# Attention's weighted sums as two column-tile products of 128x64 instead of one product of 128x128

## The chip, the core and the metric

The kernel runs on one core of a Trainium2 chip. A core has five engines with an instruction stream each: TensorE (PE in the profile, with its weight loads listed apart as PEld), VectorE (DVE), ScalarE (ACT), GpSimd (POOL) and SyncE (SP). TensorE multiplies with an array of 128 rows by 128 columns: a weight load puts a stationary matrix of up to 128x128 into it, and a MATMUL streams the columns of a second matrix through it and writes or adds the product to PSUM. The array can also be addressed as smaller tiles; a product is then told which rows and columns of the array it uses. The metric is the device time of one execution in microseconds (us), the median over runs.

## The reference, cut to what matters

One block of group norm, attention over the 32x32 pixels of an image, a projection and a residual, in float32, for 16 images of 512 channels:

```python
xn = group_norm(x, 8 groups)                              # x: (16, 512, 32, 32)
qkv = einsum('oc,bchw->bohw', qkv_w, xn) + qkv_b
q, k, v = to_heads(split(qkv, 3))                         # 4 heads of 128, n = 1024 pixels
attn = softmax(einsum('bhnd,bhmd->bhnm', q, k) * 128 ** -0.5)
out = einsum('bhnm,bhmd->bhnd', attn, v)
return x + einsum('oc,bchw->bohw', proj_w, out) + proj_b
```

The change concerns the einsum that makes `out`.

## The kernel before, in words

**Attention.** The work goes through 16 images x 4 heads x 8 key blocks of 128 pixels: 512 steps. A step has two halves of 512 query pixels. `scores` (product in L846) multiplies a key block with half of the queries, which gives scores transposed: key pixels on the partitions, 512 queries along them. ScalarE takes their exponential into the tile `p` (L852), without subtracting a maximum. `weighted_sum` (product in L942), one step later, multiplies the block of V (128 key pixels by 128 channels of the head, the stationary matrix) with the half of `p` (the streamed matrix, 512 columns) and accumulates over the 8 key blocks in `po`, a PSUM tile of 128 channels by 1024 queries. After the eighth block ScalarE copies `po` out (L949). VectorE adds the `p` tiles up (L860) for the softmax's denominators, which are divided out of the copied result later.

**V's block.** `v_block` returns it. For the first image its 128 channels lie next to each other. From the second on V comes in a layout in which the channels of one block are four elements apart: `v[:, j // n, h % 2, :, j % n]` with n = 4.

**The other products.** Q, K, V and the projection are made by two levels of Strassen's method: products of 128x128 weights with 256 streamed columns (L606; `qk_x`, `qk_y`, `v_x`, `v_y`, `pp_x`, `pp_y` in the profile) whose results are copied and added by ScalarE and VectorE. The last image's projection has one level, with 512 columns (L1031; `lx`, `ly`, `lz`).

**The order.** Python lists of such units are spread over the eight steps of a head (`plan_head`): while a head's attention runs, the projection of the image before or the Q, K or V of the next one is made between the products of the attention. In the loop at the end of `fast_path` a half step issues `scores`, then `weighted_sum` of the step before, then half of the step's units; a scheduler orders each engine's stream under the dependencies from there, so that a product of L846, one of L942 and some of L606 usually alternate on TensorE.

**Other tile shapes.** At the end a check of the softmax's range makes two products with one column and one streamed element: L1077 (32 rows) uses a 32x32 tile of the array and L1078 (128 rows) a tile of 128x32; both write `most`. All else uses 128x128. A general path for inputs out of that range is in the program and is not run here.

Of the kernel before, what the change touches and what calls it, by code (L numbers as in the profile page):

```python
# [16 lines left out]
P = 128  # L17
# [169 lines left out]
def fast_path(ctx, tc, x, sources, out, consts, flag, dims):  # L187
# [6 lines left out]
    nc = tc.nc  # L194
    B, C, N, NCC, NH2, NB, GC, SCALE = dims
# [597 lines left out]
    def v_block(b, h, j):  # L793
        v, n = vs[b, h // 2], NB // NH2
        return v[:, h % 2, j, :] if b == 0 else v[:, j // n, h % 2, :, j % n]
# [39 lines left out]
    ps, tot, po, rinv, last_eviction = {}, {}, {}, {}, {}  # L835
# [3 lines left out]
    def where(s):  # L839
        bh, j = divmod(s, NB)  # L840
        return (*divmod(bh, HEADS), j)
# [95 lines left out]
    def weighted_sum(s, half):  # L937
        b, h, j = where(s)
        if j == 0 and half == 0:
            po[b, h] = ps_o.tile([P, N], F32, tag="o", name=f"po_{b}_{h}")  # L940
        i = ts(half, HALF)
        nc.tensor.matmul(  # L942
            po[b, h][:, i], v_block(b, h, j), ps[s][:, i],
            start=(j == 0), stop=(j == NB - 1),
        )
        if j == NB - 1:
            if (b, h) not in os_:
                os_[b, h] = opool.tile([P, N], F32, tag="o", name=f"o_{b}_{h}")
            last_eviction[b] = nc.scalar.copy(os_[b, h][:, i], po[b, h][:, i])  # L949
# [291 lines left out]
    for s in range(steps + 1):  # L1241
        units = []
        if s < steps:
            b, h, j = where(s)
            if j == 0:
                plan = plan_head(b, h)
            units = plan[j]
            if j == NB - 1 and h == 2 and b + 1 < B:
                next_v.append(v_groups(b + 1))
                next_qk.append(qk_groups(b + 1, 1))  # L1250
                units.append(ahead[f"v_{b + 1}"])
        if NB < s < steps and s % NB == 1:
            denominators(*where(s - 2)[:2])
        for half in range(NH2):
            if s < steps:
                scores(s, half)
                if j in (1, 2) and half == 1 and s > NB:
                    with tc.issue_after(exps[s].ins):
                        spread_inverse(*where(s - NB)[:2], j - 1)
                if half == 1 and j == 4 and s > NB:  # L1260

                    with tc.issue_after(added[b, h, 4].ins):
                        divide(*where(s - NB)[:2])
            if s > 0:
                weighted_sum(s - 1, half)
            n = (len(units) + 1) // 2
            run(units[half * n : (half + 1) * n])
        if s > 0:
            del ps[s - 1]
# [134 lines left out]
```

## Time and profile before

| | |
|---|---|
| time, median of 2 runs | 3171.86 us (3171.75 to 3171.98) |
| span of the profiled execution | 3170.7 us |
| VectorE busy | 2633.6 us, 83% |
| ScalarE busy | 1439.7 us, 45% |
| probabilities L852, ScalarE, 1024 of 128x512 | 597 ns each |
| adding up L860, VectorE, 385 of 128x1024 | 1218 ns each |
| L606 products qk_x with qk_t, rows of 256 columns | 1344, 382 ns each |
| granted TensorE clock | full, in all of 40 slices |

The profile is of one execution. An f32 product shows as two MATMUL rows and two weight loads, so that the 1024 products of L942 are 2048 rows. A matmul's row lasts from its start to its modelled end, which lies after the start of the next; the distance of starts, and not the length of a row, is what a product takes of TensorE. In the groups of part 5 the columns are line, engine, operation, output <- inputs, array rows*columns, shape and type, count, then busy us and mean ns, then the engine's idle time before them and what ended it. The chain of part 4 is followed back from the last instruction to what released each step.

### The profile page before, as it was taken

To read this page: it belongs to the slowest core of one execution; us is meant where nothing else is said; L and a number is where in the kernel's file an instruction comes from. 1 tells how busy PE (TensorE), PEld (TensorE's weight loads), DVE (VectorE), ACT (ScalarE), POOL (GpSimd) and SP (SyncE) were. 2 spreads that over 40 slices of the span, in tenths; PEclk is the share of its full clock that TensorE was granted. 3 is DMA by queue.
4 is the path that set the end of the run, shared out by engine and by line. 5 is a ranking of instruction groups with operands and counts; after the bars stand their busy time and mean duration, and the time that the engine had idled before them with its cause. 6 is when DMAs were issued, how large, how long until landed. Compare 5 with 4: busy or idle time off the path is not lost.

```text
span 3170.7 us, 34267 instructions
## 1 busy us (share of the span) xinstructions
PE 3159.9 (100%) x10524; PEld 2190.7 (69%) x10524; DVE 2633.6 (83%) x4639; ACT 1439.7 (45%) x2712; POOL 517.7 (16%) x898
## 2 busy tenths in 40 slices
PE   9999999999999999999999999999999999999999
PEld 7566676677766676777767767677676776766764
DVE  9878879788897888878788787987879978788784
ACT  3535435354353543545435453453534545344342
POOL 0011221111211112211122111222012221122200
PEclk9999999999999999999999999999999999999999
DMA  5554554555545455454554545555455564555531
GB/s 177 185 190 154 188 172 154 171 153 192 171 164 162 153 185 175 167 167 145 191 172 162 171 145 187 171 172 172 144 175 169 176 189 134 174 162 186 179 116 41
DMA packets 210333, 524.32 MB, mean 165 GB/s; under 512 B 32096, under 2 KB 65376, under 8 KB 210144
## 3 DMA queue, kind: packets, MB, share of 16 engines
q1 hardware_dynamic: 132896, 282.12, 28.8%
q0 software_dynamic: 64000, 204.54, 19.2%
q10 hardware_dynamic: 13248, 35.39, 3.5%
q8 instruction: 87, 1.43, 0.2%
q14 instruction: 102, 0.84, 0.1%
HBM read 388.77 MB, written 133.17 MB: 165 GB/s over the span
## 4 chain that ended last, share of the span: by engine, by line
PE 96%; DVE 3%; DMA 0%; issue 0%; POOL 0%; SPq 0%; ACT 0%; DVEq 0%; POOLq 0%
PE po L942 27%; PE s L846 27%; PE qk_x L606 12%; PE qk_y L606 9%; PE pp_x L606 6%; PE v_x L606 6%; PE pp_y L606 4%; PE v_y L606 4%; PE lx L1031 0%; DVE qk_t L574 0%; PE ly L1031 0%; PE warm L1153 0%; DVE tot L860 0%; DVE qk L714 0%; DVE qk_r L630 0%
## 5 line engine op out<-in xcount | busy, mean ns | idle before, releaser
L942 PE MATMUL po<-p,v 128*128 128x512 f32 x2048 | 1049.5, 594 | 0.7 <-ACT p L852 0.7
L846 PE MATMUL s<-qk,qk 128*128 128x512 f32 x2048 | 1047.4, 593 | 0.3 <-DVE qk L714 0.3
L852 ACT ACTIVATE p<-s 128x512 f32<-128x512 f32 x1024 | 610.9, 597 | 961.0 <-PE s L846 957.2
L942 PEld LDWEIGHTS po<-p,v 128*128 128x128 f32 x2048 | 603.6, 302 | 322.7 <-issue 214.5
L860 DVE TENSOR_TENSOR tot<-tot,p 128x1024 f32<-128x1024 f32 x385 | 469.0, 1218 | 158.4 <-ACT p L852 156.3
L846 PEld LDWEIGHTS s<-qk,qk 128*128 128x128 f32 x2048 | 387.7, 190 | 88.6 <-issue 29.9
L606 PEld LDWEIGHTS qk_x<-qk_t,w 128*128 128x128 f32 x1344 | 251.8, 190 | 166.1 <-issue 75.3
L606 PE MATMUL qk_x<-qk_t,w 128*128 128x256 f32 x1344 | 356.3, 382 | 0.1
L486 ACT COPY qk_u<-qk_x 128x512 f32<-128x512 f32 (+1 forms) x256 | 136.3, 533 | 229.2 <-PE qk_x L606 229.2
L779 POOL DMA_DIRECT2D vd<-vu x120 | 66.7, 557 | 899.8 <-DVE vu L771 897.9
L630 DVE TENSOR_TENSOR qk_r<-qk_y,qk_u 128x512 f32<-128x512 f32 (+1 forms) x256 | 157.7, 616 | 34.7 <-ACT qk_u L486 21.6
L580 POOL DMA_DIRECT2D kept_t<-qk_t x240 | 129.4, 540 | 278.4 <-DVE qk_t L574 211.9
L606 PEld LDWEIGHTS pp_x<-pp_t,w_proj 128*128 128x128 f32 x630 | 117.2, 190 | 74.7 <-issue 32.3
L784 POOL DMA_DIRECT2D v<-vd x240 | 140.6, 593 | 167.1 <-DMA vd<-vu 70.3
L630 DVE TENSOR_TENSOR v_r<-v_y,v_u 128x512 f32<-128x512 f32 (+1 forms) x120 | 76.0, 633 | 110.6 <-ACT v_u L486 80.3
L606 PE MATMUL pp_x<-pp_t,w_proj 128*128 128x256 f32 x630 | 167.8, 383 | 0.0
L606 PE MATMUL v_x<-v_t,w_v 128*128 128x256 f32 x630 | 166.6, 381 | 0.0
L830 POOL DMA_DIRECT2D out_y<-y x120 | 66.0, 550 | 604.2 <-DVE y L829 602.4
L606 PEld LDWEIGHTS v_x<-v_t,w_v 128*128 128x128 f32 x630 | 118.4, 190 | 55.3 <-issue 19.1
L606 PE MATMUL qk_y<-x,w 128*128 128x256 f32 x512 | 142.1, 379 | 0.0
L714 DVE SCALAR_TENSOR_TENSOR qk<-qk_r,qkb_sb,qk_r 128x512 f32<-128x512 f32 x192 | 137.5, 743 | 1.6
L486 ACT COPY v_u<-v_x 128x512 f32<-128x512 f32 (+1 forms) x124 | 66.3, 535 | 157.1 <-PE v_x L606 130.3
(217 smaller groups left out, 4487.2 us busy)
## 6 DMA issues: line engine op xcount, KB each, us to landing
w<-kept SPq DMA_DIRECT2D x90, 512.0 KB, 3.7
kept_t<-qk_t POOLq DMA_DIRECT2D x180, 256.0 KB, 3.3
v_t<-kept_t SPq DMA_DIRECT2D x180, 256.0 KB, 2.9
w<-kept SPq DMA_DIRECT2D x90, 384.0 KB, 3.4
rinv<-row ACTq DMA_DIRECT2D x63, 512.0 KB, 4.9
x<-in_x POOLq DMA_DIRECT2D x60, 512.0 KB, 4.6
vd<-vu POOLq DMA_DIRECT2D x120, 256.0 KB, 3.1
v<-vd POOLq DMA_DIRECT2D x240, 128.0 KB, 4.2
```

The source lines that it names most:

```text
L486: nc.scalar.copy(t[n][:, :width], t["x"][:, :width])
L580: nc.gpsimd.dma_start(t, to)
L606: nc.tensor.matmul(acc[:, ts(i, Q)], have["w"][t][:, i, slot, :], inner(i, bn), start=(first and i == 0), stop=True, skip_group_check=True,)
L630: nc.vector.tensor_add(dst, view(a), view(c))
L714: nc.vector.scalar_tensor_tensor(st[b, h][:, ts(half, HALF)], a, qkb_sb[:, i : i + 1], c, ALU.add, ALU.add)
L779: nc.gpsimd.dma_start(rows[which][ts(h, P), :], u)
L784: nc.gpsimd.dma_start(vs[b, pair][ts(q, BLK), half].rearrange("m h (k i) j -> m (h k) (i j)", k=n), rows[which].rearrange("(k m) (q e) -> ...
L830: nc.gpsimd.dma_start(out[b, ts(o, P), ts(half, HALF)], t)
L846: nc.tensor.matmul(sc, ks[b, h][:, ts(j, P)], qs[b, h][:, ts(half, HALF)], start=True, stop=True)
L852: exps[s] = nc.scalar.activation(ps[s][:, ts(half, HALF)], sc, AF.Exp, scale=SCALE)
L860: added[b, h, j] = nc.vector.tensor_add(tot[b, h][:, i], tot[b, h][:, i], ps[s][:, i])
L942: nc.tensor.matmul(po[b, h][:, i], v_block(b, h, j), ps[s][:, i], start=(j == 0), stop=(j == NB - 1),)
```

## The change

`weighted_sum` takes the 128 channels of V's block as two halves of 64. Each half is a product of its own: 128 rows by 64 columns of weights, the same 512 streamed columns, and the lower or upper 64 partitions of the same stretch of `po`. The first half is placed on the array's columns 0 to 63, the second on 64 to 127. Starts and ends of the accumulation are as before, for each half by itself.

```diff
         i = ts(half, HALF)
-        nc.tensor.matmul(
-            po[b, h][:, i], v_block(b, h, j), ps[s][:, i],
-            start=(j == 0), stop=(j == NB - 1),
-        )
+        v = v_block(b, h, j)
+        for d in range(2):
+            cols = ts(d, P // 2)
+            nc.tensor.matmul(
+                po[b, h][cols, i], v[:, cols], ps[s][:, i],
+                start=(j == 0), stop=(j == NB - 1),
+            )
         if j == NB - 1:
```

In the program built from it the two halves of a product stand next to each other on TensorE in 1009 of 1024 cases; in 15 the scheduler puts another product between them (L606, once L88). The line of the product becomes L945, and later lines move by three. The other engines have the same instructions as before.

## The prediction

> **What bounds the kernel now.** I read four views, from the whole to the single instruction. First the page: the busy shares (its part 1), the chain that ended last (part 4), and the two groups of the attention in part 5.
>
> ```profile
> PE 3159.9 (100%) x10524; PEld 2190.7 (69%) x10524; DVE 2633.6 (83%) x4639; ACT 1439.7 (45%) x2712; POOL 517.7 (16%) x898
> ...
> PE po L942 27%; PE s L846 27%; PE qk_x L606 12%; PE qk_y L606 9%; PE pp_x L606 6%; PE v_x L606 6%; PE pp_y L606 4%; PE v_y L606 4%; PE lx L1031 0%; DVE qk_t L574 0%; PE ly L1031 0%; PE warm L1153 0%; DVE tot L860 0%; DVE qk L714 0%; DVE qk_r L630 0%
> ...
> L942 PE MATMUL po<-p,v 128*128 128x512 f32 x2048 | 1049.5, 594 | 0.7 <-ACT p L852 0.7
> L846 PE MATMUL s<-qk,qk 128*128 128x512 f32 x2048 | 1047.4, 593 | 0.3 <-DVE qk L714 0.3
> ```
>
> The reader is to see that TensorE (PE) alone sets the end: it has work all the time, po, the line that is changed, carries 27% of the chain, and in the whole run it waited 0.7 us for its probabilities. Nothing that lengthens po can hide. There are 1024 weighted products (16 images, 4 heads, 8 key blocks, 2 halves) and 2048 rows: an f32 product is two passes here, each a weight load and a MATMUL.
>
> A row of 594 ns is not what a pass costs, since passes overlap. The chain in order of time (start, length) gives the pitch:
>
> ```profile
> 1500.28 0.86 PE s L846 x2
> 1501.13 0.95 PE pp_x L606 x4
> 1502.08 0.87 PE po L942 x2
> 1502.95 0.86 PE pp_y L606 x4
> ```
>
> Two passes over 512 columns take 0.86 us, so one takes 0.43; four over 256 take the same, so 0.215: the time goes with the streamed columns, and the other 0.16 us of a row lies under the next pass. Check: 2048 x 0.43 = 881 us is 27.8% of the span, as the chain says.
>
> Weight loads (PEld) are hidden under the pass before, and the rows of the two lines (shortest/median/longest ns) say what one costs when it is not:
>
> ```profile
> L942 PEld LDWEIGHTS po<-p,v x2048: 186/308/332, 61.8 to 3136.9; 128*128 128x128 f32 x187
> L942 PE MATMUL po<-p,v x2048: 592/592/800, 61.8 to 3137.3; 128*128 128x512 f32 x187
> ...
> L846 PEld LDWEIGHTS s<-qk,qk x2048: 186/190/192, 60.0 to 3133.3; 128*128 128x128 f32 x187
> L846 PE MATMUL s<-qk,qk x2048: 592/592/697, 60.0 to 3133.7; 128*128 128x512 f32 x187
> ```
>
> The longest row of s is 697 - 592 = 105 ns over the usual: a pass that stood waiting for 128 weight columns. For po it is 208; its loads are slower (308 against 190) because from the second image on V lies with a stride of four elements.
>
> Last, the only place where this kernel uses another tile of the array than 128x128, the two one-element products of the final check (L1077 on a 32x32 tile, L1078 on 128x32), between full products (L1031). TensorE alone, in order of time:
>
> ```profile
> 3157.14 0.59 PE L1031 MATMUL lx<-ot,wl 128*128 128x512 f32 x1
> 3157.67 0.19 PE L1077 MATMUL most<-ones,total 32*1 32x1 f32 x2
> 3157.78 0.19 PE L1078 MATMUL most<-ones_sq,span_last 128*1 128x1 f32 x2
> 3157.90 0.70 PE L1031 MATMUL lx<-ot,wl 128*128 128x512 f32 x1
> ```
>
> The first lx pass is done streaming at 3157.14 + 0.43 = 3157.57, yet the next load starts at 3157.66 (PEld's row in the same stretch), 0.09 late, though the VectorE result it waits for was there at 3157.37. The second most pass starts at 3157.67 + 0.19 - 0.16 = 3157.70, L1078's load comes at 3157.78 (0.08); its second pass starts at 3157.81, lx's load comes at 3157.90 (0.09), and that lx row then lasts 0.70, 0.11 over the usual. So a change of tile shape costs here some 0.09 us of emptied array, and then the next weight load in the open, since it was not taken ahead.
>
> **The change, part by part.** *Work.* Each of the 1024 products becomes two, of 64 weight columns each, over the same 512 streamed columns: 4096 passes for 2048. Streaming time goes with the streamed columns, and no row has a narrow product with a long stream; I take 0.43 us for a narrow pass too. Bounds: half of that, if width counted (a rival below), and 0.43 (nothing in the trace makes a smaller product slower).
>
> *Overlap.* The passes stand in the program as tile 0 first pass, tile 0 second, tile 1 first, tile 1 second. In all of this trace TensorE's passes start in the program's order. If two column tiles can stream together but starts stay in order, tile 1's first pass cannot start before tile 0's second, which has to wait for its own tile: only the two middle passes overlap, and a product takes three slots, 1.29 us for 0.86. No row shows two tiles at work together; the bounds are two slots (full overlap) and four (none), and I take three, since order is what the rows do show.
>
> The TensorE page of the Trainium skill (TensorE: Matmul & The Clock Gate, Part 3, The mechanism) says that matmuls start and end in strict program order; that is three slots, and by its packing model, a pass and about 4 ns per further tile, it would be two; no run here shows either.
>
> *Tile changes.* In the changed program's instruction order the narrow products stand in 1007 runs of two, 30 of one (15 products have a full product of another unit put between their halves) and one of four: 1038 runs, each entered from and left to full products. Entering costs 0.09 plus the first load in the open: 64 columns, half of 208 = 0.104 (bounds 0 and 0.208). Leaving costs 0.09 plus the 0.105 that s and the L606 products show (190 ns loads). Together 0.389 us a run, 1038 x 0.389 = 404 us. Bounds: 0.16 a run (166 us) if loads were still taken ahead, 0.49 (509 us) with the upper bound of the first load; I take 0.389, as lx after most had its load in the open.
>
> The Trainium skill (TensorEngine Tiling (Array Packing), Key Properties) has it that changing the tiling mode, not just the tile, drains TensorE; by that rule the 404 us stand, without it they fall away, and the three places above agree with it at 0.08 to 0.09 us each.
>
> *Slots.* At three: 1007 x 3 + 30 x 2 + 5 = 3086 slots against 2048, 1038 more, x 0.43 = 446 us.
>
> *What costs nothing.* The other three narrow loads of a product (about half of 308 ns) lie under passes of 0.43. VectorE, ScalarE, GpSimd and SyncE have the same instructions; VectorE's order shifts at places, but with 83% of 3171 us it has room, and more in a longer run. If that cover went, VectorE's 2634 us would still be under TensorE's. No wait on another engine is added: the two halves take the semaphores of the one before, and the eviction of po is unchanged. There is hardly a stall to give back: TensorE's named waits in this profile add up to 5 us.
>
> Sum: 3170.7 + 404 + 446 = 4020.7 us of span; the median of the runs is 3171.86, 1.2 above the span, so 4022 us, 27% slower.
>
> **The rivals.** *Full overlap:* each tile has its own order, so tile 1 starts as soon as its weights are in. Slots: 1007 x 2 + 60 + 4 = 2078, 30 more, 13 us; tile 1's first load stands behind both loads of tile 0, so it trails by 0 to 0.208 us on 1009 adjacent products, 0 to 210 us. With 404 for the changes: 3589 to 3799 us. For it: the two tiles share neither columns nor output partitions. Against: every start in the trace is in order. The Trainium skill (TensorEngine Tiling (Array Packing), Key Properties) says that tiles operate independently and can load and multiply in parallel; by it the time would be this one, and no run here shows it.
>
> *No overlap:* four slots, 2048 x 0.43 = 881, and 404: 4457 us. For it: nothing here has shown two passes streaming at once. Against: only that the columns are separate.
>
> *Cheap changes:* the array changes shape without loss among large products and overlap is full: 3172 + 13 = 3185 us, no change. Against: the 0.09 us were paid after a full 512-column lx as after the tiny ones.
>
> *Faster:* a pass of 64 columns streams in half the time, 0.215 us, and the tiles overlap fully. Then a product takes 0.43, saving 0.43 x 1009 = 434 us: 2738 if the changes are free, 3142 at 404. It is faster by 2% as long as a run pays under (434 - 63) / 1038 = 0.36 us. Against: time follows the streamed columns in every row, and 0.39 is measured.
>
> **How the numbers follow.** Three slots 0.42; full overlap 0.25; no overlap 0.22; another slower case (dearer drains, tiles in each other's way, over 4480) 0.03; cheap changes 0.04; faster 0.04. The likeliest one's own range, by the bounds of the tile changes, is 3784 to 4127 us. For 8 in 10 the range has to take in the cases on both sides of it: 3590 to 4480, the upper bound of the tile changes without overlap (4562) left out. Some 2% (63 us) is what can be told from no change here: slower 0.92, same 0.04, faster 0.04.
>
> **What would show it.** In the profile after: 4096 rows of po of 128*64, with TensorE still at 100%. In order of time, tile 1's first row starting with tile 0's second shows three slots; with tile 0's first, full overlap; 0.43 after tile 0's second, none. The first narrow load should start 0.09 after the last full pass has streamed, and the first full row after a run should last about 0.105 over its usual. If full rows follow narrow ones without that, the 404 us are wrong; if narrow rows stand closer than 0.43 on one tile, the pass is.

## The result, and the profile after

| | before | after |
|---|---|---|
| time, median of 2 runs | 3171.86 us | 3597.07 us (3597.05 to 3597.08) |
| ratio | | 1.1337, 95% interval 1.1304 to 1.137 |
| span of the profiled execution | 3170.7 us | 3595.3 us |
| passes of po | 2048 | 4096 |

The change makes the kernel 425 us slower, half of the 850 us that were forecast. First the page of the changed kernel: busy shares, chain, and po's passes and weight loads (columns as before).

```profile
PE 3586.9 (100%) x12572; PEld 1827.2 (51%) x12572; DVE 2669.0 (74%) x4639; ACT 1449.8 (40%) x2712; POOL 508.7 (14%) x898
...
PE po L945 31%; PE s L846 25%; PE qk_x L606 12%; PE qk_y L606 9%; PE pp_x L606 6%; PE v_x L606 6%; PE v_y L606 4%; PE pp_y L606 4%; PE lx L1034 0%; DVE qk_t L574 0%; DMA x<-in_x 0%; PE ly L1034 0%; DVE qk_r L630 0%; PE pv L88 0%; DVE qk L714 0%
...
L945 PE MATMUL po<-p,v 128*64 128x512 f32 x4096 | 1179.8, 646 | 0.7 <-ACT p L852 0.7
...
L945 PEld LDWEIGHTS po<-p,v 128*64 128x64 f32 x4096 | 323.9, 200 | 708.9 <-issue 689.9
```

TensorE still sets the end, and po has twice the passes; but 4096 rows of 0.646 us cover only 1180 us of the engine's time. One after the other at a pitch of 0.43 they would have covered at least 1761, so they lie on top of each other. The chain in order of time shows what a product takes:

```profile
1701.67 0.86 PE s L846 x2
1702.53 0.43 PE pp_x L606 x2
1702.96 1.07 PE po L945 x4
1704.03 1.06 PE s L846 x2
1705.09 1.07 PE po L945 x4
1706.16 0.63 PE pp_x L606 x2
```

Four narrow passes take 1.07 us where two full ones took 0.86, and the first full product after them takes 0.20 more than elsewhere (1.06 against 0.86 for s, 0.63 against 0.43 for pp_x). How the four lie is seen in TensorE's rows in order of time, three short stretches of time around one product, one below the other (each answer lists the rows that touch its stretch), and in the weight loads:

```profile
1702.58 0.38 PE L606 MATMUL pp_x<-pp_t,w_proj 128*128 128x256 f32 x1
1702.89 0.71 PE L945 MATMUL po<-p,v 128*64 128x512 f32 x2
...
1703.43 0.60 PE L945 MATMUL po<-p,v 128*64 128x512 f32 x2
...
1703.96 0.70 PE L846 MATMUL s<-qk,qk 128*128 128x512 f32 x1
```

```profile
1702.89 0.32 PEld L945 LDWEIGHTS po<-p,v 128*64 128x64 f32 x4 [0.33 <-issue]
1703.96 0.30 PEld L846 LDWEIGHTS s<-qk,qk 128*128 128x128 f32 x2 [0.75 <-issue]
```

Two passes of 0.70 us start within 0.01 of each other at 1702.89, the other two within 0.01 at 1703.43; in all 1007 runs of one product the second row starts 6 or 7 ns after the first. Rows on one and the same tile follow each other 0.43 us apart, as s shows for full products and the second experiment below for narrow ones, so each pair is one pass of either tile: two slots, not three. Before the pair 1702.58 + 0.215 = 1702.795, when pp_x has streamed, to 1702.89 is empty (0.09); the first two of the four loads start 6 ns apart and last 0.19 us each, and all four come in 0.32 us, so the two tiles load at the same time as well. At the end the last passes have streamed at 1703.44 + 0.43 = 1703.87, the next load starts at 1703.96 (0.09 again), and s lasts 0.70 instead of 0.59.

### The profile page after: what moved, and what is told of

The parts are those of the page before. It is cut to its first block, busy times and chain, and to the rows that moved or that the text cites. A ratio compares the mean times of both kernels' runs of the same rounds, so it can differ in the third digit from the quotient of the medians.

```text
span 3595.3 us, 38320 instructions
## 1 busy us (share of the span) xinstructions
PE 3586.9 (100%) x12572; PEld 1827.2 (51%) x12572; DVE 2669.0 (74%) x4639; ACT 1449.8 (40%) x2712; POOL 508.7 (14%) x898
## 4 chain that ended last, share of the span: by engine, by line
PE 98%; DVE 1%; DMA 0%; issue 0%; SPq 0%; ACTq 0%; ACT 0%; DVEq 0%
PE po L945 31%; PE s L846 25%; PE qk_x L606 12%; PE qk_y L606 9%; PE pp_x L606 6%; PE v_x L606 6%; PE v_y L606 4%; PE pp_y L606 4%; PE lx L1034 0%; DVE qk_t L574 0%; DMA x<-in_x 0%; PE ly L1034 0%; DVE qk_r L630 0%; PE pv L88 0%; DVE qk L714 0%
## 5 line engine op out<-in xcount | busy, mean ns | idle before, releaser
L945 PE MATMUL po<-p,v 128*64 128x512 f32 x4096 | 1179.8, 646 | 0.7 <-ACT p L852 0.7
L846 PE MATMUL s<-qk,qk 128*128 128x512 f32 x2048 | 1060.1, 599 | 0.1
L945 PEld LDWEIGHTS po<-p,v 128*64 128x64 f32 x4096 | 323.9, 200 | 708.9 <-issue 689.9
L846 PEld LDWEIGHTS s<-qk,qk 128*128 128x128 f32 x2048 | 377.6, 190 | 141.0 <-ACT p L852 48.7
L606 PE MATMUL qk_x<-qk_t,w 128*128 128x256 f32 x1344 | 386.4, 404 | 0.1
L606 PEld LDWEIGHTS qk_x<-qk_t,w 128*128 128x128 f32 x1344 | 227.9, 189 | 278.5 <-ACT p L852 170.6
L606 PE MATMUL pp_x<-pp_t,w_proj 128*128 128x256 f32 x630 | 177.5, 398 | 0.0
L606 PE MATMUL v_x<-v_t,w_v 128*128 128x256 f32 x630 | 174.4, 393 | 0.0
L630 DVE TENSOR_TENSOR qk_r<-qk_y,qk_p 128x512 f32<-128x512 f32 (+1 forms) x128 | 79.2, 619 | 124.3 <-PE qk_y L606 124.1
L606 PEld LDWEIGHTS pp_x<-pp_t,w_proj 128*128 128x128 f32 x630 | 109.5, 189 | 111.1 <-ACT p L852 25.5
L606 PEld LDWEIGHTS v_x<-v_t,w_v 128*128 128x128 f32 x630 | 112.2, 189 | 84.4 <-ACT p L852 56.6
L606 PE MATMUL qk_y<-x,w 128*128 128x256 f32 x512 | 148.4, 391 | 0.0
```

Source lines behind the costliest of these rows:

```text
L606: nc.tensor.matmul(acc[:, ts(i, Q)], have["w"][t][:, i, slot, :], inner(i, bn), start=(first and i == 0), stop=True, skip_group_check=True,)
L630: nc.vector.tensor_add(dst, view(a), view(c))
L846: nc.tensor.matmul(sc, ks[b, h][:, ts(j, P)], qs[b, h][:, ts(half, HALF)], start=True, stop=True)
L945: nc.tensor.matmul(po[b, h][cols, i], v[:, cols], ps[s][:, i], start=(j == 0), stop=(j == NB - 1),)
```

## The experiments

TensorE shows no tile in its rows, and ends of matmuls are modelled. So the overlap that the starts show had to be tested, and with it what the 425 us are: the change of shape, or the narrow products themselves. The second, third, fourth and sixth experiment were run once each, the others four to ten times; a loss or gain against the kernel before is taken from its runs beside them (medians of 3171.92, 3172.54 and 3172.41 us).

**All products narrow.** A helper takes the place of every product with 128 weight columns in the fast path, except the group norm's and the warm-up.

```diff
+    def matmul(to, w, moving, **flags):
+        for d in range(2):
+            cols = ts(d, P // 2)
+            ins = nc.tensor.matmul(to[cols], w[:, cols], moving, **flags)
+        return ins
```

> All products of the fast path with 128 weight columns (attention, Q, K, V, projection, last projection) become pairs of 128x64 column tiles; only the group norm's small products, the warm-up and the final check keep other shapes, so that the array changes shape some 35 times to narrow and back and not 1038. Theory A (each tile works through its own passes side by side with the other; the whole loss is the change of shape, 0.41 us a run): the loss goes away, 35 x 0.41 = 14 us over the kernel before, 3175 to 3200 us. Theory B (a pair of narrow products itself is dearer than the full one by about 0.4 us): 5196 pairs x 0.4, over 5000 us.

Measured: 3307.44 us, ratio 1.0427 (1.041 to 1.0445). Five times as many products are narrow as in the changed kernel, and two thirds of the loss are gone: theory B falls. But theory A expected 3175 to 3200. TensorE's waits show where to look (waiter, released by, us in all, times, longest):

```profile
PE qk_x L203 <- ACT qk_u L493: 23.8, 49, 0.6
PE v_x L203 <- ACT v_u L493: 9.3, 15, 0.6
PE pp_x L203 <- ACT pp_u L493: 4.3, 15, 0.4
PE v_y L203 <- DVE v_r L637: 4.2, 15, 0.4
```

In the kernel before, the same question names no wait for such a copy. A count over the whole trace says how much there is of it. Each pass is taken to stream for 0.429 us (half of that at 256 columns) from its start, or later by what its row lasts over the usual. By this count the array was empty for 63 us more than before, and for 141 us only one of its halves streamed. As half an array is half a loss, that is 63 + 141 / 2 = 134 us, all by which the profiled execution is longer. The scheduler had given twice as many products another order, with products next to what they wait for and the halves of a pair apart. That this order is the cause is tested in the fifth and the seventh experiment.

**Both halves on one tile.** The counterpart of the overlap.

```diff
             cols = ts(d, P // 2)
+            at = cols if j == 0 else ts(0, P // 2)
             nc.tensor.matmul(
-                po[b, h][cols, i], v[:, cols], ps[s][:, i],
-                start=(j == 0), stop=(j == NB - 1),
+                po[b, h][at, i], v[:, cols], ps[s][:, i],
+                start=(j == 0), stop=(j == 0 and d == 1) or (j == NB - 1 and d == 1),
             )
```

> From the second key block on, both halves of V go to the same column tile (they are added into the lower 64 partitions, so the result is wrong); the number of products, their shapes and the changes of shape stay as in the changed kernel. Theory A (two tiles side by side, each pass 0.43 us): the 881 products that stood beside each other now take four slots for two, 881 x 2 x 0.43 = 758 us more, about 4350 us. Theory C (the tiles do not overlap, but a narrow pass takes half the time, 0.215 us; the trace's ends are only modelled): no change, about 3597 us.

Measured: 4346.59 us, 750 over the changed kernel. A product in this kernel's chain:

```profile
1702.64 1.92 PE po L946 x4
```

1.92 against 1.07: four slots against two. (The edit moves the tile and the output partitions together.) So the tiles do stream at the same time, and a narrow pass costs the full 0.43; theory C, and with it the halved pass of the prediction's fourth rival, is out.

**Runs of four.** The same narrow products in 592 runs instead of 1038, and so with fewer changes of shape.

```diff
-            if s > 0:
-                weighted_sum(s - 1, half)
+            if s > 0 and half == 1:
+                weighted_sum(s - 1, 0)
+                weighted_sum(s - 1, 1)
```

> The two weighted sums of a step are issued one after the other, after the second scores, so that most runs hold four narrow products: 592 runs for 1038, the same 2048 narrow products, 36 slots more than the kernel before. Theory A: 3172 + 592 x 0.405 + 36 x 0.43 = 3172 + 240 + 15, about 3427 us. If the loss were in the narrow products and not in the changes of shape: about 3597 us.

Measured: 3422.4 us. The loss is 250 us for 592 runs, 425 for 1038: it goes with the runs. Without the slots of split products, 15 and 13 us, it is 0.40 us a run in both. One run in the chain:

```profile
1700.80 1.93 PE po L945 x8
```

**Tile 0 first.** `weighted_sum` makes both halves of a step, with the loop over the tiles outside and the loop over the two stretches of queries inside.

```diff
+        for d in range(2):
+            cols = ts(d, P // 2)
+            for half in range(NH2):
+                i = ts(half, HALF)
...
```

> As the runs of four, but within a run both products of tile 0 stand before both of tile 1: four passes of tile 0, then four of tile 1; 528 runs, 36 slots more than before. Own order for each tile, with a queue that reaches past four passes: 3172 + 528 x 0.405 + 15, about 3400 us. Starts in program order, or a look ahead of only one or two passes: tile 1 starts with tile 0's last pass, seven slots for four, 494 x 3 x 0.43 = 637 us more, about 4040 us, or in between.

Measured: 3402.66 us. The chain's row of one run:

```profile
1713.78 1.93 PE po L946 x8
```

Eight passes take the same 1.93 us as in the third experiment, where the tiles alternate, though here four passes of tile 0, with their loads, stand ahead of tile 1's first. By the starts tile 1 begins 0.013 or 0.014 us after tile 0, in all 493 such runs. So each tile works through its own passes; the program's order between the tiles does not hold it back over at least four. How far beyond that it reaches was not tried.

**All narrow, TensorE's order as before.** The products are recorded as they are made and bound, pair after pair, to the order in which they stand in the kernel before (order alone, no wait).

```diff
+    for i, k in zip(order, order[1:]):
+        tc.add_manual_dep(
+            MADE[k][0], MADE[i][1].name,
...
+            reason="order of before",
+        )
```

> As the first experiment (all 128-column products as pairs of column tiles), but TensorE's products are bound to the order that the kernel before has, both halves of each next to each other; the first one came to 3307 us with the steady stretches as dense as before, and with the array half or wholly empty for 134 us more at places where the scheduler had another order. Theory A (only the changes of shape cost): some 35 changes x 0.41 = 14 us, 3180 to 3200 us. Theory B (a pair is dearer than a full product, by 130 / 5196 = 0.025 us each): 3307 us again.

Measured: 3215.25 us, 1.0133 (1.0116 to 1.015): 93 of the 136 us were TensorE's order, and 43 stayed, more than theory A's 8 to 28. The waits:

```profile
PE v_y L214 <- DVE v_r L650: 16.3, 30, 0.9
PE po L214 <- ACT o L969: 8.9, 14, 0.6
```

They are for other results of VectorE and ScalarE, whose own orders still differed. Neither theory was settled by this run.

**Four tiles.** `range(4)` and `P // 4` in the loop of the change.

> The weighted sums as four products of 128x32 in four column tiles; everything else as in the changed kernel. 1053 runs, 60 slots more than the kernel before. Theory A, by its terms: 0.094 until the array is empty, a first load of 32 columns in the open, half of the 0.112 seen for 64, 3 x 0.008 until the fourth tile starts, 0.094 and 0.105 for leaving: 0.373 a run, 1053 x 0.373 = 393, and 60 x 0.43 = 26, less some 11 us of stalls given back: about 3580 us. If the load in the open costs the same for 32 columns as for 64, 59 us more: about 3640. If tiles overlapped two at a time only: another 1006 x 0.86 = 865 us more.

Measured: 3570.36 us, 27 less than with two tiles although there are 15 more runs.

```profile
1700.66 1.03 PE po L945 x8
```

Eight passes in 1.03 us: four tiles stream at the same time; in the trace their first loads, and their first passes, start within 0.02 us. The rows of the line (shortest, median and longest ns), first of the changed kernel, then of this one:

```profile
L945 PE MATMUL po<-p,v x4096: 592/593/705, 61.8 to 3561.9; 128*64 128x512 f32 x196
```

```profile
L945 PE MATMUL po<-p,v x8192: 592/593/650, 62.5 to 3535.2; 128*32 128x512 f32 x200
```

The longest, which waited for its load, is 113 ns over the usual with 64 columns and 58 with 32: the load in the open halves with the columns.

**All narrow, all orders as before.** VectorE and ScalarE are bound to their orders in the same way.

> As the fifth experiment (all 128-column products as pairs, TensorE in the order of the kernel before), and now VectorE and ScalarE are bound to their order in the kernel before too; the fifth had 1% over the kernel before, in waits for VectorE and ScalarE, whose order the scheduler had changed. Theory A (a pair costs what the full product costs; the 1% came from the other order): what is left are 34 small products of the group norm at 128x128, each with one change to and from narrow, 0.24 us over what they have in the kernel before: 8 us, about 3180 us. Theory B (pairs are dearer by 0.008 us each): about 3215 us again.

Measured: 3171.17 us, 0.9995 (0.9985 to 1.0004), no difference. Its chain:

```profile
1701.77 0.86 PE s L217 x4
1702.62 0.43 PE pp_x L217 x4
1703.05 0.86 PE po L217 x4
```

A pair takes what the full product took: 0.86 at 512 columns, 0.43 at 256. Theory B is out. The zero is a balance of small things, 9 us under the 3180 expected: counted as in the first experiment, the array was empty for 12 us less than before, and one of its halves streamed alone for 22 us more.

**The group norm narrow too.** `pm` and `pv` become pairs as well.

> As the seventh, and the group norm's small products are pairs of column tiles as well, so that the array keeps its shape from the warm-up to the final check. Theory A: the 8 us go away, 3168 to 3175 us, the same as the kernel before. Theory B: 3210 us.

Measured: 3162.39 us, 0.9969 (0.9958 to 0.998): 10 us faster than the kernel before, more than expected, and the fastest kernel here. By the starts of po's passes the head in which the next image's norm is made takes 49.39 us before, 49.60 in the seventh and 49.05 here (median of 14 images). That is some 8 us less than in the seventh, as theory A has it for this step, and some 5 less than before. Counted as above, the array was empty for 22 us less than before and half of it streamed alone for 22 us more, which comes to 11 us; why the other gaps shrink was not taken apart.

**The change alone, all orders as before.** Only the weighted sums narrow.

> The change alone (only the weighted sums narrow), with TensorE, VectorE and ScalarE bound to the order of the kernel before, both halves of a product always next to each other: 1023 runs, no product split. Theory A, by the terms seen in the changed kernel (0.094 to empty, 0.112 first load, 0.008 trailing, 0.094 to empty, 0.105 first load back): 1023 x 0.413 = 422, less 64 x 0.06 for the first image's faster loads, 418: about 3590 us, 7 less than the changed kernel, whose 15 split products cost 15 x 1.25 = 19 and which had some stalls to give back.

Measured: 3579.7 us, 1.1281 (1.1262 to 1.13): 407 over the kernel before, with every engine's instructions in the order of before and no product split. Its chain:

```profile
1701.67 1.07 PE po L220 x4
1702.74 1.06 PE qk_x L215 x4
1703.80 0.86 PE qk_y L215 x4
```

This is the price of 1023 changes of shape and back: 0.40 us each, near the 0.413 of its terms.

## Why the prediction was wrong

*The bound* was right: TensorE at 100% before and after, the other engines' instructions as before, nothing hidden. In the ninth experiment, which moves nothing, the loss is the change itself.

*The overlap* is the step that failed. It bounded a product by two and four slots and took three, "since order is what the rows do show". What the rows show, but for two one-element products, is passes that all use the same 128 columns; their order says nothing of two tiles side by side. The runs put the lower bound in its place: two slots, 0.43 + 0.43, with the second tile 0.007 to 0.013 us behind (changed kernel, fourth experiment), and four only where both halves go to one tile (second). The 446 us for 1038 slots shrink to 13, for the 15 products that the scheduler split. The Trainium skill's sentence that matmuls start in strict program order (TensorE: Matmul & The Clock Gate, Part 3, The mechanism) differs from these starts, since tile 1 starts before passes of tile 0 that stand ahead of it, in the fourth experiment before a whole product; that the tiles operate independently (TensorEngine Tiling (Array Packing), Key Properties) agrees with them. The measurement decides.

*The rival of full overlap* was the right mechanism, at 3589 to 3799 us. Its spread, tile 1 trailing by up to 0.208 us behind tile 0's loads, was not needed: the loads of the two tiles run at the same time, and the time lies 8 us above its lower end. That it lies so near is in part a balance: counted as in the first experiment, the changes of shape took 415 us and not 404, the second tile's 0.007 us came to some 8, and stalls gave back 10. That 3597 us lies inside the stated range, 7 us from its lower end, is owed to the range having been drawn over this rival, and not to the three slots.

*The changes of shape* were sized rightly from three places in the whole trace of before. Entering was 0.194, and is 0.094 + 0.112, the second because 64 strided columns take a bit more than half of 0.208; in the first image, where V is not strided, the longest row is 643 ns, 51 over the usual. Leaving was 0.195, and is 0.094 + 0.105. With 0.41 for 0.389, 1038 runs come to 426 and the split products' 13 make 439; 425 were measured. The first image accounts for some 4 of the difference; the other 10, which the ninth experiment has too, are stalls given back: counted as before, the array was empty away from the changes of shape for 44 us before, 33 in the changed kernel and 35 in the ninth. That these gaps close because TensorE is slower is argued, not shown. The prediction had "hardly a stall to give back", as it counted TensorE's named waits alone, 5 us; this term was mis-sized.

*A narrow pass at 0.43* was right (second experiment), and so was that weight loads within a run cost nothing. *Cheap changes* fell: 0.40 us each. *Faster by halved passes* fell as well.

## What to carry to other kernels

Before a product is cut into tiles of the array, count how often the array's shape changes, not how many products there are: here each change to 64 columns and back cost some 0.40 us whether the run held four passes or eight, while the tiles themselves cost nothing. If tiles are wanted, give them to all products in the neighbourhood, and keep their order. And an order that a trace shows for one resource is no evidence for two; where no row shows the pair, keep the cases apart instead of taking the middle.

## What the runs showed that was not expected

Each tile takes its passes in its own order, past at least four passes of the other tile that stand ahead, and the loads of two or four tiles run at the same time (four loads of 0.19 us in 0.32, the first two 6 ns apart). With the order held, cutting every product into halves cost nothing (0.9995), and with the norm's small products it gained 10 us. The first of these kernels lost 136 us, and all of that went away with the order in which the scheduler had put the same work.
